# A four-layer graph stack on one core: TensorE's order written out for the third layer, with its side work cut into steps

## The chip, the cores and the metric

The kernel runs on one core of a Trainium2 chip. The metric is the device time of one execution in microseconds. Five engines work in parallel, each through its own queue in order: TensorE (PE in the profile, its weight loads PEld), VectorE (DVE), ScalarE (ACT), GpSimd (POOL) and SyncE (SP, which here only issues transfers). They wait for each other through semaphores.

## The reference

Four graph layers in a row over 4096 nodes with 256 features, all in float32. Each one adds an attention result to x and normalises every row (`x = layernorm(x + layer(x, adj))`). Which nodes see each other is given by a 4096 x 4096 integer matrix `adj`.

- Layer 0: additive attention with four heads, slope 0.2, then elu.
- Layer 1: dot-product attention with four heads of 64.
- Layer 2, the third layer: additive attention with one head:

```
h = x @ W;  e_src = h @ a[:D, 0];  e_dst = h @ a[D:, 0]
e = leaky(e_src[:, None] + e_dst[None, :], 0.01)
out = elu(softmax(where(adj > 0, e, -1e12), axis=1) @ h)
```

- Layer 3, the fourth layer: attention whose scores are cosines. `Qn` and `Kn` are the rows of `x @ Wq.T` and `x @ Wk.T` divided by their lengths, and the output is half the attended x plus half of x.

## The kernel before, in words

All of x stays in SBUF as `X`, 32 tiles of 128 nodes with 256 columns and one more for the sums. A row block is 512 nodes (`QW`), so there are `NB` = 8 row blocks b and `NT` = 32 column tiles j. The names below are those of the profile's lines.

**The third layer** (`additive_one`) goes through its units (b, j) with b outside and j inside. For a unit, `weights` loads the masks of two units with one transfer on SP's queue (L428), has ScalarE form `e` from the block's `row` (L430) and has VectorE multiply with the mask into `prob` (L432, three buffers). `sums` then does four matmuls, one for each 128 nodes of the block (L438), which add up in four PSUM banks over all j: for even b in banks of their own (`acc0` to `acc3`), for odd b in the rotating banks `g`. The loop emits `sums` of a unit one step after its `weights`.

Before it can use column tiles of a block, the block must be *prepared*: `turn` transposes its x tiles (L118) through two banks, VectorE and ScalarE copy one each into `xT` (L120), `additive_values` multiplies xT with the layer's weights in four banks (L177), and from each bank ScalarE takes three exponentials (L181 to L183) and VectorE the scaled values V (L184). Last, `row` of the block is filled: for blocks 0 and 1 by four transposes of `src` and a copy (L420, L421), for the later ones by two transfers on POOL's queue (L415, L416). Blocks 0 and 1 are prepared ahead of the loop and the others during row block 0, one every four units (at j = 2, 6, 10 and so on), each in one piece.

**The second layer's last outputs** (`tail` of `multi_head_attention`) are done inside the third layer, after `sums(0, 2)`: POOL adds the partial row sums (`join_sums`, L646), TensorE sums them over partitions (L658), ScalarE copies them (`kept`, L661), TensorE turns them (L666) and the outputs (L673), VectorE divides, adds to X and normalises. After it, `follow.start` opens the fourth layer's buffers and loads its weights.

**The fourth layer's preparations** (`Cosine.prepare`) for blocks 0 to 5 are done in the third layer's last row block (b = 7, at j = 2, 6 and so on) in the banks `acc` that are then free, and for blocks 6 and 7 in the fourth layer's first row block (at j = 1 and 12). Each turns x (L118), projects each of its four tiles (L795, two tiles share one bank), squares them with a running sum (`sq`, L799), copies a bank to `rows` (L801), works out the inverse root (L130 to L140), scales `rows` (L806), transposes them (L810) and copies the result to `T` (L811). Its main work is scores (L834), exponential (L837), mask (L838) and sums (L845).

**What sets the order.** In the first two layers TensorE's order is written out by hand (`tc.manual_schedule`). In the third and fourth a planner orders every engine's instructions by its own costs; the program's order is then a starting point. A tile that comes from a pool waits until the readers of the tile that had its buffer before are done.

## Time and profile before

| | us |
|---|---|
| median of three runs (2927.59 to 2929.03) | 2928.59 |
| the profiled execution's own time | 2932.88 |
| its span, first to last instruction | 2931.0 |
| third layer's front in it, 1724.5 to 1803.7 | 79.2 |
| its row blocks with no side work on TensorE, to 2154.9 | 351.2 |
| its last row block, to 2246.9 | 92.0 |
| fourth layer's front, to 2296.0 | 49.1 |

A line of the order in time has the start, the duration from the first start to the last end of a group of neighbours, engine, line, operation, output and inputs, the count, and in brackets the idle time before it with the engine and line that ended it. A float32 matmul leaves two records, a transpose one. Because matmuls are pipelined, a record's duration is longer than the distance to the next record's start. A line of the waits reads: who waited, for whom, microseconds in total, number of times, the longest.

### The profile page before, as it was taken

What the parts mean: (1) busy time and instruction counts of PE and PEld (TensorE: products, weight loads), DVE (VectorE), ACT (ScalarE), POOL (GpSimd) and SP (SyncE); (2) the same over time, 40 slices, a digit from 0 to 9 for tenths busy, and PEclk for the clock granted to TensorE, in tenths of its full rate; (3) what the DMA queues carried; (4) which work ended last, traced back from release to release, by engine and by line L of the source; (5) the groups of instructions that cost most, each with busy time, mean ns of one, the idle gap of its engine ahead of it and who ended that gap; (6) DMA issues with size and microseconds to landing.
All of it is one profiled execution on the core that took longest, in us unless ns stands there. A gap on an engine that the chain in (4) does not pass through costs nothing.

```text
span 2931.0 us, 50407 instructions
## 1 busy us (share of the span) xinstructions
PE 2909.7 (99%) x20269; PEld 1560.3 (53%) x20269; DVE 1958.3 (67%) x2545; ACT 1668.9 (57%) x2613; POOL 926.6 (32%) x647
## 2 busy tenths in 40 slices
PE   9999999999999999999999999999999999999998
PEld 4333333333643333333333358888887777777776
DVE  8899999997677777877877865555555333333333
ACT  7899999997356666666666654444444222222222
POOL 0010010100078888888889850000000000000000
PEclk9999999999999999999999999999999999999999
DMA  7566666664068888889889876444442333333331
GB/s 203 102 138 139 136 141 141 137 131 84 1 147 191 183 185 190 182 185 195 176 187 188 180 161 137 151 152 151 154 132 52 51 58 58 58 58 58 58 58 29
DMA packets 207148, 374.94 MB, mean 128 GB/s; under 512 B 15057, under 2 KB 90817, under 8 KB 206018
## 3 DMA queue, kind: packets, MB, share of 16 engines
q0 software_dynamic: 102304, 177.77, 38.3%
q1 hardware_dynamic: 104336, 193.69, 20.1%
q8 instruction: 159, 2.61, 0.4%
q14 instruction: 75, 0.61, 0.1%
q10 hardware_dynamic: 274, 0.26, 0.0%
HBM read 317.07 MB, written 21.04 MB: 115 GB/s over the span
## 4 chain that ended last, share of the span: by engine, by line
PE 96%; DVE 2%; ACT 0%; DMA 0%; SPq 0%; issue 0%; DVEq 0%; ACTq 0%
PE acc L274 23%; PE acc L845 15%; PE p L604 14%; PE acc L637 14%; PE g L438 8%; PE acc L438 8%; PE p L834 4%; PE g L834 3%; PE g L532 2%; PE g L177 1%; PE pv L546 1%; PE acc L795 1%; PE g L118 1%; DVE prob L616 1%; DVE s L139 1%; PE acc L177 1%
## 5 line engine op out<-in xcount | busy, mean ns | idle before, releaser
L616 DVE TENSOR_TENSOR prob<-p,mask 128x1024 f32<-128x1024 f32 x512 | 622.8, 1222 | 197.4 <-ACT p L606 193.6
L606 ACT ACTIVATE p<-p,shift 128x1024 f32<-128x1024 f32 x512 | 556.3, 1088 | 331.8 <-PE p L604 331.0
L274 PE MATMUL acc<-prob,V 128*32 128x512 f32 x6144 | 664.0, 592 | 1.1 <-DVE prob L264 1.1
L623 POOL TENSOR_TENSOR den<-den,prob 128x1024 f32<-128x1024 f32 x248 | 618.5, 2494 | 72.1 <-DVE prob L616 62.7
L261 ACT ACTIVATE prob<-row,dst 128x512 f32<-128x512 f32 x1020 | 633.1, 712 | 0.1
L264 DVE SCALAR_TENSOR_TENSOR prob<-prob,mask 128x2048 f32<-128x2048 f32 x256 | 582.4, 2286 | 24.2 <-ACT prob L261 20.6
L604 PE MATMUL p<-qT,kT 64*64 64x512 f32 x4096 | 532.7, 591 | 5.5 <-DVE prob L616 5.5
L637 PE MATMUL acc<-prob,V 64*64 64x512 f32 x4096 | 531.4, 589 | 0.0
L845 PE MATMUL acc<-X,prob 128*128 128x257 f32 x2048 | 486.0, 380 | 0.0
L845 PEld LDWEIGHTS acc<-X,prob 128*128 128x128 f32 x2048 | 388.4, 190 | 162.2 <-issue 113.5
L838 DVE TENSOR_TENSOR prob<-prob,mask 128x512 f32<-128x512 f32 x256 | 176.3, 691 | 419.5 <-ACT prob L837 418.4
L274 PEld LDWEIGHTS acc<-prob,V 128*32 128x32 f32 x6144 | 197.3, 110 | 453.0 <-issue 433.5
L91 POOL COPY tick<-prob 128x1 f32<-128x1 f32 x35 | 39.7, 1133 | 1019.9 <-DVE prob L264 646.0
L430 ACT ACTIVATE e<-row,dst 128x512 f32<-128x512 f32 x256 | 184.3, 721 | 241.2 <-DVE prob L432 208.4
L637 PEld LDWEIGHTS acc<-prob,V 64*64 64x64 f32 x4096 | 155.8, 133 | 285.4 <-issue 278.2
L604 PEld LDWEIGHTS p<-qT,kT 64*64 64x64 f32 x4096 | 153.6, 133 | 284.4 <-issue 255.8
L432 DVE SCALAR_TENSOR_TENSOR prob<-e,mask 128x512 f32<-128x512 f32 x256 | 178.3, 696 | 174.7 <-PE acc L438 92.9
L782 POOL DMA_DIRECT2D mask<-in_adjT x64 | 47.4, 741 | 639.5 <-DVE prob L838 509.7
L629 POOL DMA_DIRECT2D den<-prob x240 | 225.2, 938 | 28.5 <-DVE prob L616 21.9
L837 ACT ACTIVATE prob<-p 128x512 f32<-128x512 f32 x144 | 85.8, 596 | 256.7 <-PE p L834 242.7
L438 PE MATMUL g<-V,prob 128*128 128x257 f32 x1024 | 226.6, 380 | 0.0
L438 PE MATMUL acc<-V,prob 128*128 128x257 f32 x1024 | 225.3, 380 | 0.0
(154 smaller groups left out, 1973.7 us busy)
## 6 DMA issues: line engine op xcount, KB each, us to landing
mask<-in_adjT SPq DMA_DIRECT2D x256, 512.0 KB
den<-prob POOLq DMA_DIRECT2D x240, 512.0 KB, 5.3
mask<-edges SPq DMA_DIRECT2D x256, 128.0 KB
mask<-in_adjT POOLq DMA_DIRECT2D x64, 512.0 KB, 5.7
edges<-in_adj POOLq DMA_DIRECT2D x32, 512.0 KB, 9.9
den<-prob SPq DMA_DIRECT2D x16, 512.0 KB
row<-far SPq DMA_DIRECT2D x7, 1024.0 KB
X<-in_x SPq DMA_DIRECT2D x7, 512.0 KB
```

Of the source, the lines that this page charges most:

```text
L261: nc.scalar.activation(z[:, h, :], r, AF.Relu, bias=-1.0, scale=dst[:, j, h:h + 1])
L264: nc.vector.scalar_tensor_tensor(z, z, 1.0, mask[m][:, j % MJ, :].unsqueeze(1).to_broadcast([P, H, QW]), OP.add, OP.mult)
L274: nc.tensor.matmul(acc[b][h * G:(h + 1) * G, n, :], part, prob[b, j][:, h, :], start=(j == 0), stop=(j == NT - 1))
L438: nc.tensor.matmul(acc[b][k][:, :D + 1], prob[b, j][:, k * P:(k + 1) * P], V[:, j, :], start=(j == 0), stop=(j == NT - 1))
L604: nc.tensor.matmul(p[c * d:(c + 1) * d, r, :], kT[half, c, j * d:(j + 1) * d], qT[half, c, cols], start=True, stop=True)
L606: nc.scalar.activation(p, p, AF.Exp, bias=shift)
L616: nc.vector.tensor_tensor(z, p, mask[m][:, j % MJ, :].unsqueeze(1).to_broadcast([P, KC, QW]), OP.mult)
L623: nc.gpsimd.tensor_tensor(to, to, flat, OP.add)
L629: nc.gpsimd.dma_start(to, flat, accum_op=OP.add)
L637: nc.tensor.matmul(acc[b][c][r * d:(r + 1) * d, :], V[half, j, r * d:(r + 1) * d], prob[b, j][half, r, :], start=(j == 0), stop=(j == NH - 1))
L834: nc.tensor.matmul(p, T[:, 0, j * P:(j + 1) * P], T[:, 1, cols], start=True, stop=True)
L845: nc.tensor.matmul(acc[b][k], prob[b, j][:, k * P:(k + 1) * P], X[:, j, :], start=(j == 0), stop=(j == NT - 1))
```

## The change

TensorE's order in the third layer is now the program's own, through `tc.manual_schedule`; the other engines are still ordered by the planner. The program's order is changed with it:

- `prepare` of the third layer is split into `turn`, `project` and `fill_row`. A block's `turn` is emitted at j = 0, 4, 8 and so on, its `project` and `fill_row` two units later. In front of the loop, the projection of block 1 is split around the filling of row 0, and row 1 is filled after `sums(0, 1)`.
- `tail` of the second layer has three steps: POOL's additions after `sums(0, 0)`, the row sums after `sums(0, 3)`, the rest after `sums(0, 5)`, there with all transposes ahead of the reciprocals. `follow.start` comes after the last step. The tile for the row sums is taken where they are made.
- `Cosine.prepare` has three steps, at units 0, 2 and 5 of a period of four in the last row block and at (0, 1), (0, 3), (0, 6) and (0, 12), (0, 14), (0, 17) in the fourth layer: turn; projections, squares, root and scaling; transposes to T. In the middle step both tiles of a bank are projected before the first of them is squared.

```diff
+            with tc.manual_schedule(engines={mybir.EngineType.PE}):
+                xTs = {0: turn(0), 1: turn(1)}
+                project(0, xTs[0])
+                project(1, xTs[1], [0, 1])
+                fill_row(0)
+                project(1, xTs[1], [2, 3])
+                for i in range(len(units) + 1):
+                    if i < len(units):
+                        b, j = units[i]
+                        weights(b, j)
+                        if b == 0 and j // QB + 2 < NB:
+                            n = j // QB + 2
+                            if j % QB == 0:
+                                xTs[n] = turn(n)
+                            elif j % QB == 2:
+                                project(n, xTs[n])
+                                fill_row(n)
+                    if i:
+                        b, j = units[i - 1]
+                        sums(b, j)
+                        if (b, j) == (0, 1):
+                            fill_row(1)
+                        if b == 0 and j in (0, 3, 5):
+                            tail(bank, (0, 3, 5).index(j))
+                            if j == 5:
+                                follow.start()
...
+                            for step, first in enumerate((0, 2, 5)):
+                                if j >= first and (j - first) % 4 == 0 and (j - first) // 4 < NB - 2:
+                                    follow.prepare(even_bank, (j - first) // 4, step)
...
-        def tail(bank):
+        def tail(bank, step):
             b = NB - 1
-            join_sums(b, 1, nc.gpsimd)
-            join_sums(b, 2, nc.gpsimd)
-            row_sums(bank, b)
-            reciprocals(turned_row_sums(bank, b), b)
-            for k in (0, 2):
-                half(turned_half(bank, b, k), b, k)
...
+            if step == 0:
+                join_sums(b, 1, nc.gpsimd)
+                join_sums(b, 2, nc.gpsimd)
+            elif step == 1:
+                row_sums(bank, b)
+            else:
+                pd = turned_row_sums(bank, b)
+                pos = {k: turned_half(bank, b, k) for k in (0, 2)}
+                reciprocals(pd, b)
+                for k, po in pos.items():
+                    half(po, b, k)
...
+            if step == 0:
+                self.xT[b] = transposed_block(in_, bank, b)
+            elif step == 1:
...
+                for k in range(0, QB, 2):
                     pr = bank().rearrange("p (t n f) -> p t n f", t=2, f=P)
+                    for t in range(2):
+                        for c in range(KC):
+                            nc.tensor.matmul(pr[:, t, :, :], xT[:, c, (k + t) * P:(k + t + 1) * P], w_sb[:, c, :],
+                                             start=(c == 0), stop=(c == KC - 1))
+                    for t in range(2):
+                        for n in range(2):
+                            sq = in_.tile([P, P], FP, name="sq")
+                            nc.scalar.activation(sq, pr[:, t, n, :], AF.Square, accum_out=norm[:, k + t, n:n + 1])
+                    nc.vector.tensor_copy(rows[:, k:k + 2], pr)
...
+            steps = {(0, j + n): (NB - 2 + b, step) for b, j in enumerate((1, 12)) for step, n in enumerate((0, 2, 5))}
...
+                    if (b, j) in steps:
+                        co.prepare(bank, *steps[b, j])
```

## The prediction

> **What bounds the kernel now.** I read the page's busy times and its chain first: is one engine the limit, and where does it rest?

> ```profile
> PE 2909.7 (99%) x20269; PEld 1560.3 (53%) x20269; DVE 1958.3 (67%) x2545; ACT 1668.9 (57%) x2613; POOL 926.6 (32%) x647
> PE 96%; DVE 2%; ACT 0%; DMA 0%; SPq 0%; issue 0%; DVEq 0%; ACTq 0%
> ```

> TensorE is busy nearly all of the span and is 96% of the chain that ended last. So nothing is gained by making another engine faster; only TensorE's own standstills can be won. The matmul count is unchanged by the edit. Next, the windows table by stage (columns: PE, PEld, DVE, ACT, POOL busy with counts, granted clock, DMA share, GB/s), cut where the third layer's front (preparations in row block 0), its middle, its last row block and the fourth layer's front begin and end:

> ```profile
> 1724.50:1803.70 79.20, 77.08 (x405) 64.90 (x402) 42.67 (x87) 33.34 (x134) 11.55 (x12) 1.00 0.54 123
> 1803.70:2154.90 351.20, 351.20 (x1621) 307.37 (x1620) 196.20 (x430) 157.37 (x243) 1.83 (x3) 1.00 0.47 153
> 2154.90:2246.90 92.00, 91.67 (x450) 74.31 (x449) 51.86 (x123) 46.63 (x162) 3.54 (x7) 1.00 0.36 92
> 2246.90:2296.00 49.10, 48.68 (x204) 35.10 (x203) 26.32 (x66) 19.97 (x64) 2.22 (x3) 1.00 0.23 33
> ```

> The clock is 1.00 in all four, so it is no issue. Busy time misleads here: records of neighbouring matmuls overlap (each is 0.38 us long but the next starts 0.22 later), so a standstill under 0.2 us doesn't show as idle. I therefore count from start to start. TensorE's order in time gives the undisturbed pace:

> ```profile
> 1803.62 18.38 PE L438 MATMUL acc<-V,prob 128*128 128x257 f32 x84
> 1821.84 28.35 PE L438 MATMUL g<-V,prob 128*128 128x257 f32 x130
> ```

> 84 records in 18.22 us: 0.217 each (a float matmul leaves two records, a transpose one). In the same way L177 and L795 run at 0.217 and 0.216 where nothing holds them, and transposes at 0.109. Multiplying:
> - Front, from the first transpose (1724.51) to 1803.62: 172 records of L438 = 37.3, 128 of L177 = 27.9, 84 transposes (L118, L420, L666, L673) = 9.2, L658 = 0.6; sum 75.0. It took 79.1: **about 4.2 us stand still** (adding up single gaps gives 4.4).
> - Last row block, 2154.92 to 2246.89: 256 of L438 = 55.5, 96 of L795 = 20.7, 96 transposes = 10.5; sum 86.7. It took 92.0: **5.3** (gap by gap 5.6).
> - Fourth layer's front to 2296: gap by gap **1.7**.
> - The middle: 0.5 over 351 us, nothing to win.

> What ends these standstills is in the chain of waits, window 1690 to 2300, for TensorE and its weight loads:

> ```profile
> PE g L177 <- DVE xT L120: 1.9, 1, 1.9
> PE g L666 <- ACT kept L661: 0.2, 1, 0.2
> PEld acc L795 <- ACT sq L799: 3.9, 12, 0.4
> PEld acc L795 <- ACT xT L120: 1.7, 6, 0.4
> PEld g L795 <- ACT sq L799: 1.6, 4, 0.7
> ```

> A weight load that waits 0.2 to 0.4 is partly covered by the matmul still running; about 0.1 us shows on TensorE for each.

> **Part 1: block 2's turn two units ahead of its projection.** The one long wait, in order of time:

> ```profile
> 1736.46 2.34 POOL L646 TENSOR_TENSOR den<-den 128x1024 f32<-128x1024 f32 x1 [7.60 <-DMA den<-prob]
> 1736.55 2.81 DVE L432 SCALAR_TENSOR_TENSOR prob<-e,mask 128x512 f32<-128x512 f32 x1 [1.14 <-PE acc L438]
> 1739.28 0.68 DVE L120 COPY xT<-g 128x512 f32<-128x512 f32 x1
> 1740.11 3.91 PE L177 MATMUL g<-w_sb,xT 128*128 128x258 f32 x16 [1.85 <-DVE xT L120]
> ```

> VectorE's masking took 2.81 beside a usual 0.69 while POOL's addition ran; the copy of xT stood behind it, and TensorE behind the copy. In the changed order I place TensorE by its pace: turns of blocks 0 and 1 to 1726.25, project(0) to 1729.8, half of project(1) to 1731.5, row 0 to 1732.0, the other half to 1733.7, turn(2) to 1734.6, sums(0,0) to 1736.3, project(2) to 1739.8, sums(0,1) to 1741.5. VectorE in the built order: prob(0,0) ends 1734.3 (row copy 0.59 from 1732.3, e 0.72, prob 0.69), 0.3 before sums(0,0); xT(2) ends 1735.6, 0.7 before project(2); prob(0,1) then runs to 1736.3 and prob(0,2) meets POOL's addition.

> [...] By the rows, that prob ends 1739.4 at the latest, while project(2) needs none and keeps TensorE at work until 1739.8. I take 0 for it, 2.1 as the other end, and so **gain 2.0** (gap of 2.01).

> The same part also spaces the later turns (gaps of about 0.15 at each of blocks 4 to 7, 0.26 at block 2: 0.9 in all). **Gain 0.9.** Row fills inside the projections (four gaps, 0.44) go, since 4 x 0.217 x 2 of projection now lie between src and its transposes. **Gain 0.4.**

> **Part 2: the second layer's tail in three steps.** Row sums at (0,3), their transposes at (0,5): the wait for the two kept copies (0.36+0.11 start to start, and 0.1+0.1 around the sums) falls under two units of 1.73 us. **Gain 0.6.** Behind it VectorE gets reciprocals 0.3, two products 1.3, two additions 1.3, statistics of four rows 2.4, xT(4) 0.7, 6.0 in one burst before prob(0,9); from the last transposes TensorE has sums(0,6) to (0,8), turn(4) and project(4), 9.6 us, before it needs that prob: no wait. The two weight loads of SP's queue (0.37 and 0.46) wait for the row sums to free den, 1747 before and 1746.9 after by the pace; SP's list is the same, the mask behind them is for units 14 and 15, some 20 us later: 0. POOL's far and row transfers keep their order and feed row blocks from 2 on: 0.

> Front: 2.0+0.9+0.4+0.6 = **3.9** of 4.4.

> **Part 3: the fourth layer's preparations in steps, tiles of a bank ahead of squares.** One of six in the last row block:

> ```profile
> 2199.39 1.04 PE L118 MATMUL acc<-ident,X 128*128 128x128 f32 x8
> 2200.26 1.03 PE L438 MATMUL g<-V,prob 128*128 128x257 f32 x4
> 2201.13 3.07 PE L795 MATMUL acc<-w_sb,xT 128*128 128x256 f32 x12
> 2204.04 1.46 PE L438 MATMUL g<-V,prob 128*128 128x257 f32 x6
> 2205.49 1.13 PE L795 MATMUL acc<-w_sb,xT 128*128 128x256 f32 x4
> 2206.46 4.50 PE L438 MATMUL g<-V,prob 128*128 128x257 f32 x20
> 2211.01 1.06 PE L810 MATMUL acc<-ident,rows 128*128 128x128 f32 x8
> 2211.91 0.60 PE L438 MATMUL g<-V,prob 128*128 128x257 f32 x2
> 2212.34 1.04 PE L118 MATMUL acc<-ident,X 128*128 128x128 f32 x8
> ```

> From transposes to transposes 12.95 us. By the pace: 32 x 0.217 + 16 x 0.109 + 16 x 0.216 = 12.13. So 0.82 stands still: about 0.18 at xT's two halves, 0.36 at squares, 0.21 ahead of L810, the rest scattered. After: xT has two units (3.5 us) for two copies of 0.68 and 0.57: gone. A bank's eight records follow each other: gone.

> [...] The row: in the trace, the last projection's start to the end of the rows' scaling takes 4.6, with one prob in between; four squares in a row instead of two add 0.5: 5.1. The new order puts three units and a turn, 3 x 1.73 + 0.87 = 6.1, between. [...] Only the first preparation, where VectorE also does block 6's four outputs, comes out late. Its queue, from the block's start: first output and the taking of block 6 to 2.6, xT and probs 2 to 4 to 5.6, the other outputs (1.5 each, waiting for ScalarE's exponentials) around the copies of rows, which end at 12.6, prob(7,6) to 13.5, root to 14.5, scaling to 15.8; TensorE arrives at 15.6. With 0.2 to start, **0.4 is lost** (0 to 1.0). Gain in the last row block: 5.6 less 0.4 there, less 0.1 left of scattered gaps = **5.1**.

> In the fourth layer the planner still places TensorE. Steps at units 1, 3, 6 and 12, 14, 17 cover the same waits: of 1.7, I take **1.3** (0.5 to 1.7), as VectorE also finishes the third layer there.

> **Sum.** 3.9+5.1+1.3 = 10.3 of the profiled execution, whose time was 2932.88 (span 2931.0): 0.351%. The runs' median is 2928.59, 0.15% below it; the same share gives **2918.3 us**.

> **Rivals.**
> 1. [...] If prob(0,0) or xT(2) is still unserved at 1736.5 (0.9 of delay does it), project(2) or sums(0,1) waits as before: 2.1 back, and some 0.5 more where probs run late behind it: 2920.9. For it: the margins of 0.3 and 0.7 at sums(0,0) and project(2) are thin. Against: the addition's start is set by a transfer, not by VectorE.
> 2. *Short gaps are the price of a first weight load behind a wait, satisfied or not.* Then only the long ones go (2.0, 0.5, L810's 0.2 x 6, fourth layer 0.7): 4.4, so 2924.2. For it: gaps of 0.104 to 0.105 recur at every bank. Against: L438 waits for a prob in every unit of the middle and shows no gap.
> 3. *VectorE's chain to the rows becomes the bound: slower.* TensorE's order is now rigid; where before other matmuls were put in front of a late rows tile, it would stand. Each of eight preparations would pay what the chain exceeds 6.1 by; from 1.3 us of excess each, all 10.3 are gone, and at 2.2, a chain of 8.3, it is 2935.9. Against: VectorE has 6.9 us of work in 12.1 there (four probs 2.8, three copies 2.1, scaling 1.2, five small 0.8).
> 4. *The edit is void for other engines*, as it fixes TensorE alone. But the built order of VectorE and ScalarE does follow: xT's copy stands two or three probs ahead of its projection's values.

> **How the numbers follow.** The likeliest has 0.73, with its own range 2916.5 (all but 0.5 of 11.7 won, 11.2, and run noise of 0.7) to 2920.5 (first preparation 1.0, fourth layer 0.5, scattered). Rival 1 has 0.12, rival 2 0.10, rival 3 0.05. About 0.2% (5.9 us) is what a measurement of this kernel can tell from no change. The likeliest and rival 1 are faster by more, rival 2 is within it, rival 3 slower: 0.85, 0.10, 0.05. The range takes in rival 1: 2916.0 to 2922.5, leaving out rivals 2 and 3 and thin tails.

> **What would show it.** After: no wait of L177 for DVE's xT above 0.2; no weight load of a projection held by squares; transposes to transposes 12.1 to 12.2 for five of six preparations; one short wait at the first rows; the middle unchanged; the fourth layer beginning some 9 earlier. A prob of 2 to 3 us beside POOL's addition will still be there, with no TensorE wait after it. It would be wrong if gaps of 0.1 stay at satisfied waits, or if new waits for prob appear behind V's values or the tail's burst.

## The result, and the profile after

| | us, median | runs |
|---|---|---|
| before, beside the first runs of the changed kernel | 2928.45 (2927.59 to 2930.18) | 6 |
| changed | 2919.78 (2918.81 to 2921.05) | 6 |
| changed kernel's profiled execution (before: 2932.88) | 2920.01, span 2918.1 | 1 |

The ratio is 0.997, 95% interval 0.9957 to 0.9983: the change makes the kernel faster by 0.3%, 8.7 us. Measured a second time, with the kernel before beside it, it was 2920.49 against 2930.47, ratio 0.9965 (0.9953 to 0.9978), 10.0 us.

The page of the changed kernel, busy times and the chain that ended last:

```profile
PE 2901.0 (99%) x20269; PEld 1564.5 (54%) x20269; DVE 1959.0 (67%) x2545; ACT 1668.3 (57%) x2613; POOL 927.0 (32%) x647
PE 97%; DVE 2%; ACT 0%; issue 0%; DMA 0%; DVEq 0%; SPq 0%
```

The same number of matmuls, and the other engines are as busy as before. TensorE still sets the end; it only stands less. The windows table of the changed kernel, cut at the four stages (columns as before: length, then busy times with counts of PE, PEld, DVE, ACT, POOL, granted clock, DMA share, GB/s):

```profile
1722.75:1801.00 78.25, 78.25 (x418) 68.56 (x415) 43.59 (x90) 33.88 (x138) 12.97 (x14) 1.00 0.49 135
1801.00:2149.30 348.30, 348.30 (x1608) 304.80 (x1608) 195.04 (x427) 156.37 (x239) 0.54 (x1) 1.00 0.47 152
2149.30:2236.00 86.70, 86.70 (x450) 76.78 (x449) 52.41 (x123) 47.13 (x161) 3.62 (x7) 1.00 0.38 98
2236.00:2285.00 49.00, 49.00 (x206) 36.85 (x205) 26.87 (x67) 18.98 (x63) 2.37 (x4) 1.00 0.23 33
```

In each stage TensorE's busy time is now the whole length (before: 77.08 of 79.20 and 91.67 of 92.00). Busy time hides short standstills, so the count from start to start decides: 0.4 us stand still in the front and 0.15 in the last row block and the fourth layer's front together, where before it was 4.4 and 7.3. In the chain of waits from 1690 to 2320 there is no line left for TensorE, and of its weight loads none that waits for xT or sq.

The front in order of time, TensorE, VectorE and POOL, at the place of the former long wait:

```profile
1731.97 1.04 PE L118 MATMUL g<-ident,X 128*128 128x128 f32 x8
...
1733.11 0.68 DVE L120 COPY xT<-g 128x512 f32<-128x512 f32 x1
...
1734.58 3.66 PE L177 MATMUL g<-w_sb,xT 128*128 128x258 f32 x16
1735.17 2.35 POOL L664 TENSOR_TENSOR den<-den 128x1024 f32<-128x1024 f32 x1 [8.07 <-DMA den<-prob]
1735.24 2.83 DVE L434 SCALAR_TENSOR_TENSOR prob<-e,mask 128x512 f32<-128x512 f32 x1 [0.25 <-ACT e L432]
```

The prob beside POOL's addition still takes 2.83 us. But xT of block 2 was copied at 1733.11, before it, and TensorE is at work on the projection until 1738.08, about when VectorE is free again.

One preparation of the last row block, TensorE in order of time, from one turn to the next:

```profile
2174.42 1.04 PE L118 MATMUL acc<-ident,X 128*128 128x128 f32 x8
2175.30 1.90 PE L440 MATMUL g<-V,prob 128*128 128x257 f32 x8
2177.03 1.04 PE L840 MATMUL acc<-ident,rows 128*128 128x128 f32 x8
2177.91 1.90 PE L440 MATMUL g<-V,prob 128*128 128x257 f32 x8
2179.64 3.62 PE L823 MATMUL acc<-w_sb,xT 128*128 128x256 f32 x16
2183.09 3.63 PE L440 MATMUL g<-V,prob 128*128 128x257 f32 x16
2186.56 1.04 PE L118 MATMUL acc<-ident,X 128*128 128x128 f32 x8
```

12.14 us from turn to turn, where it was 12.95; the undisturbed pace gives 12.13. The sixteen projections now stand in one group.

### Where the time went

By TensorE's records I cut every trace at the same events: the start of the first transpose of the third layer, of the first sums of row block 1 (the front lies between), of the first sums of row block 7 and of the first record behind the last sums of that row block, and the end of TensorE's last record. In us:

| kernel | front | middle | last row block | rest (fourth layer) | sum |
|---|---|---|---|---|---|
| before | 97.32 | 333.08 | 91.98 | 676.06 | 1198.44 |
| before, second execution (first experiment) | 99.07 | 333.08 | 92.01 | 675.91 | 1200.07 |
| changed | 93.46 | 333.08 | 86.71 | 674.06 | 1187.31 |
| changed, second execution | 93.46 | 333.08 | 86.71 | 674.06 | 1187.31 |

The changed kernel gives the same numbers to a hundredth both times. The kernel before doesn't: its front differs by 1.75 us from one execution to another. The middle, which nothing touches, is equal in all. What the two profiled executions differ by beyond the 11.1 of this table (2932.88 - 2920.01 = 12.9) lies ahead of the third layer, in code that is the same; that start lay between 1721.6 and 1724.5 us over all traces of all kernels here, and the 1724.5 is the first trace of the kernel before.

### The profile page after: what moved, and what is told of

It reads as the page before. It is cut to its first block, busy times and chain, and to the rows that moved or that the text cites. A ratio compares the mean times of both kernels' runs of the same rounds, so it can differ in the third digit from the quotient of the medians.

```text
span 2918.1 us, 50377 instructions
## 1 busy us (share of the span) xinstructions
PE 2901.0 (99%) x20269; PEld 1564.5 (54%) x20269; DVE 1959.0 (67%) x2545; ACT 1668.3 (57%) x2613; POOL 927.0 (32%) x647
## 4 chain that ended last, share of the span: by engine, by line
PE 97%; DVE 2%; ACT 0%; issue 0%; DMA 0%; DVEq 0%; SPq 0%
PE acc L274 23%; PE acc L875 15%; PE p L622 15%; PE acc L655 14%; PE acc L440 8%; PE g L440 8%; PE p L864 4%; PE g L864 3%; PE g L550 2%; PE g L177 1%; PE pv L564 1%; PE g L118 1%; PE acc L823 1%; PE acc L177 1%; DVE prob L634 1%; DVE s L139 1%
## 5 line engine op out<-in xcount | busy, mean ns | idle before, releaser
L432 ACT ACTIVATE e<-row,dst 128x512 f32<-128x512 f32 x256 | 184.2, 722 | 235.1 <-DVE prob L434 209.0
```

## The experiments

My theory: TensorE's standstills come from dependences that are too close in its order; moving the dependent work some units away removes them, and the fixing of the order is only a means. Rivals: short gaps are the price of any wait, the gain is in one part alone, the fixed order itself is what helps.

### The kernel before, once more

The kernel before, unaltered.

> The kernel before, unchanged, profiled once more. The traces differ by 11.1 us from the third layer's first transpose to the end (1206.5 before, 1195.4 after), the runs' medians by 8.7. Theory A, the trace of before is typical: that stretch is 1206.5 again, with a wait of L177 for VectorE's xT of about 1.9 us. Theory B, the wait hangs on when the transfer ahead of POOL's addition lands, and differs between executions: the stretch comes out up to 2.5 us shorter, with a smaller wait or none.

Measured 2930.82 us, ratio to the other runs of before 0.9999 (0.9991 to 1.0007). Its trace in order of time, POOL, VectorE and TensorE at the long wait:

```profile
1733.98 2.35 POOL L646 TENSOR_TENSOR den<-den 128x1024 f32<-128x1024 f32 x1 [7.65 <-DMA den<-prob]
1734.01 2.86 DVE L432 SCALAR_TENSOR_TENSOR prob<-e,mask 128x512 f32<-128x512 f32 x1 [1.14 <-PE acc L438]
...
1737.62 5.59 PE L177 MATMUL g<-w_sb,xT 128*128 128x258 f32 x16 [1.90 <-DVE xT L120]
```

and the windows of this trace over that projection (the granted clock is the third value from the end):

```profile
1737.60:1738.70 1.10, 1.08 (x3) 0.78 (x4) 0.00 (x0) 0.56 (x2) 0.00 (x0) 0.79 0.76 149
1738.70:1741.80 3.10, 3.10 (x9) 2.42 (x9) 0.69 (x2) 0.59 (x6) 0.00 (x0) 0.52 0.32 116
1741.80:1745.00 3.20, 3.20 (x16) 2.79 (x15) 1.70 (x4) 0.69 (x7) 0.62 (x1) 1.00 0.02 5
```

The same wait of 1.9 us again (idle 1.90 here, 1.85 in the first trace). The addition came 12.0 us after the layer's first transpose, as in the first trace. Yet the front was 1.75 longer, and the windows say why: behind the wait the granted clock was 0.52 for three microseconds. The projection came at half the pace, 0.43 from record to record instead of 0.217, and its sixteen records took 5.59 in place of 3.91. In the first trace of the same program the clock stayed at 1.00 there (1740.1 to 1744.3). So this one collision has no fixed price: 2.0 in one execution, 3.8 in another. Neither theory had this; the last section works out from the traces how the two executions differ.

### The front alone

The changed kernel's front (turns early, tail in steps, order fixed), with the old preparations of the fourth layer, whose row block is again ordered by the planner:

```
-                            for step, first in enumerate((0, 2, 5)):
-                                if j >= first and (j - first) % 4 == 0 and (j - first) // 4 < NB - 2:
-                                    follow.prepare(even_bank, (j - first) // 4, step)
+                            if j % 4 == 2 and j // 4 < NB - 2:
+                                follow.prepare(even_bank, j // 4)
...
+                for i in range((NB - 1) * NT):
+                    unit(i)
+            for i in range((NB - 1) * NT, len(units) + 1):
+                unit(i)
```

> The change in row blocks 0 to 6 alone (turn, project, fill_row apart, the second layer's tail in steps, TensorE's order fixed there); the fourth layer's preparations in one piece as before, ordered by the planner. Theory: the front's standstills go (4.4 to 0.4 by the trace after), so 4.0 us faster than before if the wait for xT is in every execution, 2.0 if it is not; the last row block keeps its 5.3. Rival, that VectorE's and ScalarE's planned order in the last block follows the front: it changes there too.

Measured 2927.45 us, ratio 0.9989 (0.9983 to 0.9996) to before at 2930.8: 3.35 less. Front 93.46, last row block 92.01. The whole front is won, not only its long wait, and nothing leaks into the last row block.

### The fourth layer's preparations alone

The kernel before with only the preparations in three steps and both tiles of a bank ahead of the squares; the planner orders TensorE:

```
-                    if b == NB - 1 and j % 4 == 2 and j // 4 < NB - 2:
-                        follow.prepare(even_bank, j // 4)
+                    if b == NB - 1:
+                        for step, first in enumerate((0, 2, 5)):
+                            if j >= first and (j - first) % 4 == 0 and (j - first) // 4 < NB - 2:
+                                follow.prepare(even_bank, (j - first) // 4, step)
```

> The other part alone: the fourth layer's preparations in three steps with both tiles of a bank ahead of squares, no order fixed, the front as before. Theory: 7.2 us faster than before, since the gaps of the last row block and of the fourth layer's front (7.3) go to 0.15, and the planner keeps the steps' order; the front keeps 4.4. Rival, that the fixed order is what wins there: the planner moves the projections back among the sums, and at most half of it, 3 us, is won.

Measured 2923.64 us, ratio 0.9975 (0.9965 to 0.9985): 7.16 less. Last row block 86.71, the same as in the changed kernel, with no order fixed; front 96.61, the old one. So the steps do it. The two parts add up in the traces: the front of the run above is that of the changed kernel, and so is the last row block of this one. The medians' 3.35 + 7.16 = 10.5 stands beside 8.7 and 10.0 for the whole change. Built without the fixed order, the whole changed program also comes out with the same list of instructions on all five engines: once the program's order is spaced, the planner keeps it, in the front too.

### Squares between the tiles of a bank

The changed kernel with one line left out, so that the first tile of a bank is squared before the second is projected:

```
                             for c in range(KC):
                                 nc.tensor.matmul(pr[:, t, :, :], xT[:, c, (k + t) * P:(k + t + 1) * P], w_sb[:, c, :],
                                                  start=(c == 0), stop=(c == KC - 1))
-                    for t in range(2):
                         for n in range(2):
```

> The changed kernel with each tile's squares ahead of the next tile of its bank again. In the third layer TensorE's order doesn't change, so the second tile of a bank waits for two squares of the first. Theory, by the trace of before (squares start 0.41 after the last record of a tile starts, take 0.26 + 0.36 with the read of the sum, then a weight load): 0.9 to 1.0 of standstill twice per preparation, 11 us over six, which takes back the whole change: 2930 to 2932. Rival, that a wait for squares costs only the 0.10 seen before: 2921.

Measured 2935.63 us, ratio to before 1.0017 (1.0011 to 1.0024): slower than before. In its chain of waits, and on TensorE in order of time within one preparation:

```profile
PE acc L823 <- ACT sq L827: 11.8, 12, 1.3
```

```profile
2183.16 1.03 PE L823 MATMUL acc<-w_sb,xT 128*128 128x256 f32 x4
2185.47 1.99 PE L823 MATMUL acc<-w_sb,xT 128*128 128x256 f32 x8 [1.28 <-ACT sq L827]
2188.24 1.13 PE L823 MATMUL acc<-w_sb,xT 128*128 128x256 f32 x4 [0.78 <-ACT sq L827]
```

The last row block grew by 15.0, 1.25 for each of twelve waits, not the 0.95 that I expected. The second wait of a pair is that size (start to start 0.94 over the pace), the first is 1.45, because the forming of `e` for a unit of the main work (0.72) stood ahead of the squares on ScalarE. In the kernel before the same dependence cost 0.36 for each preparation, because the planner had put sums between the tiles. A fixed order needs this edit: without it the last row block loses 15.0, more than the whole change wins.

### Rows one unit, and two units, after the projections

In the changed kernel three units lie between the projections and the transposes of the scaled rows. Two kernels with one number different:

```
-                            for step, first in enumerate((0, 2, 5)):
+                            for step, first in enumerate((0, 2, 3)):
```

> The changed kernel with one number different: in the third layer's last row block the third step (rows transposed to T) comes one unit after the projections, not three. Theory A (the distance of the steps is what hides VectorE's and ScalarE's chain): in the changed kernel this chain takes 4.97 us from the start of the last projection to the end of the scaling (5.3 in the first preparation), and about 0.15 more to TensorE's start. With one unit between them (1.75 of projection and unit, 0.2 of the last projection itself) TensorE arrives after 1.95 and stands 3.2, six times: 19 us more than the changed kernel in the last row block (86.7 becomes 105.8), some 2939 in all, slower than before by about 0.3%. Theory B (rival 3 of the prediction the other way round: the chain is short when nothing else is in VectorE's queue, so the distance does not matter): last row block 87 to 90, total within 3 us of the changed kernel, about 2920 to 2923.

Measured 2950.09 us, ratio to before 1.0063 (1.0049 to 1.0078). Its chain of waits, and its windows around one wait:

```profile
PE acc L840 <- DVE rows L834: 15.0, 5, 3.0
PE acc L840 <- DVE s L137: 3.3, 1, 3.3
```

```profile
2176.00:2182.00 6.00, 3.35 (x16) 2.61 (x14) 3.66 (x9) 3.36 (x19) 0.96 (x2) 1.00 0.32 87
2182.00:2187.00 5.00, 4.64 (x19) 4.02 (x20) 0.33 (x2) 1.17 (x2) 0.00 (x0) 0.66 0.77 108
2187.00:2194.00 7.00, 7.00 (x37) 6.23 (x36) 2.56 (x4) 3.69 (x12) 0.00 (x0) 1.00 0.37 99
```

The waits are as predicted by theory A: 3.17 from start to start, five times, and 3.47 the first time, 19.3 in all. The last row block grew by 29.6 to 116.30, though. The rest, 10.3 or 1.7 for each wait, is in the second window: the granted clock is 0.66 there and back at 1.00 in the third. After every one of the six waits nine or ten records took double their usual distance (sums 0.43 instead of 0.217).

The same number again, two units instead of three, `(0, 2, 4)`:

> The changed kernel with the third step of the preparations in the last row block two units after the projections, not three (one unit gave 116.3 us for the last row block instead of 86.7: 3.17 us of waiting each time, and behind each wait about 1.5 us more because TensorE's next records came at half the pace, the granted clock being 0.58 to 0.69 there). Between the projections and the rows lie two units and the next turn, 0.2 + 3.46 + 0.87 = 4.5 us (3.7 for the last preparation, which has no turn behind it), against a chain of 4.97 (5.28 in the first) and 0.15. Theory A (a wait costs its own length, and below about 1.3 us the clock stays up, as it did with waits of 1.25): waits of 0.9, four of 0.6 and one of 1.4, 4.7 us in all, last row block 91.4, granted clock 1.00 throughout, time about 2925. Theory B (every standstill is followed by matmuls at half the pace): 1.5 more for each wait, last row block about 100, granted clock under 0.97 there, time about 2934.

Measured 2924.93 us, ratio to before 0.9981 (0.9973 to 0.9988), last row block 91.41, and the clock 1.00. Its chain of waits:

```profile
PE acc L840 <- DVE rows L834: 2.9, 5, 1.3
PE acc L840 <- ACT xT L120: 0.7, 1, 0.7
```

Theory A holds to 0.01 us: 4.70 more than the changed kernel. Each wait is what the chain (4.97, and 0.15 to TensorE's start) exceeds the work in between by, and with these standstills, of up to 1.43, the granted clock was 1.00 over the block.

### POOL's second addition left out

The kernel before without this instruction, which leaves one part of the row sums of the second layer's last block out:

```
             join_sums(b, 1, nc.gpsimd)
-            join_sums(b, 2, nc.gpsimd)
```

> The kernel before, with one instruction left out: POOL's second addition in the second layer's last outputs (the one of 2.34 us beside which VectorE's prob took 2.81). One part of the row sums of that layer's last block is thereby missing. Everything else, TensorE's order too, is as before. Theory A (the wait of 1.9 for xT is made by that addition, through VectorE): no prob longer than 0.8 us and no wait of L177 for xT at this place; the front takes 96 to 97 us where the two looks at the kernel before took 97.3 and 99.1; time 1.5 to 2.5 us under the kernel before. Theory B (the wait is that of the turn itself: TensorE arrives too early for the copies whether or not POOL works): a wait of L177 for xT of 1 to 2 us stays, and the time is within 0.7 us of the kernel before.

Measured 2929.55 us against 2931.33, ratio 0.9995 (0.9986 to 1.0003). Its trace at the place:

```profile
1736.30 0.69 DVE L432 SCALAR_TENSOR_TENSOR prob<-e,mask 128x512 f32<-128x512 f32 x1 [1.14 <-PE acc L438]
1736.91 0.68 DVE L120 COPY xT<-g 128x512 f32<-128x512 f32 x1
1737.84 3.81 PE L177 MATMUL g<-w_sb,xT 128*128 128x258 f32 x16
```

The prob takes 0.69 and the wait for xT is gone, in TensorE's old order: the addition made the wait, through VectorE. The front is 95.21, where I expected 96 to 97. That is below the three old fronts with the addition (96.61, where the held prob took 2.09 and TensorE was idle for 1.13; 97.32; 99.07) and still 1.75 over the new one: the short gaps at the turns (0.15 each), at row fills (0.24) and at the kept copies (0.37) are there as before. By the time alone this run can't be told from no change; the trace tells it.

### The tail in one piece

The changed kernel with the second layer's last outputs in one piece again:

```
-                        if b == 0 and j in (0, 3, 5):
-                            tail(bank, (0, 3, 5).index(j))
-                            if j == 5:
-                                follow.start()
+                        if (b, j) == (0, 2):
+                            for step in range(3):
+                                tail(bank, step)
+                            follow.start()
```

> The changed kernel with the second layer's last outputs in one piece again, all three steps one behind the other after sums(0, 2), TensorE's order fixed as in the changed kernel. Theory A (part 2 of the prediction: the steps hide the kept copies): a wait of TensorE for kept comes back, 0.36 and 0.11 and two of 0.1, so the front takes 94.0 to 94.4 instead of 93.46 and the time is 0.6 to 0.9 us over the changed kernel, about 8 under the kernel before. Theory B (the tail's early position also lets VectorE's burst and POOL's addition fall on other probs, and TensorE pays for that): the front grows by 2 us or more, and new waits for prob or for POOL's den stand in it.

Measured 2921.28 us, ratio to before 0.9966 (0.9954 to 0.9979), front 94.81. The one line of its chain of waits:

```profile
PE g L685 <- ACT kept L680: 1.3, 1, 1.3
```

The mechanism is theory A's, and nothing of theory B shows; the size is 1.35 by the front instead of 0.5 to 0.9. I had taken the wait of the kernel before, where the planner had put sums of a unit between the row sums and their transposes; in a fixed order nothing stands there. The medians (0.8 over the changed kernel's second median, 1.5 over its first) are too close to tell more.

### The order fixed, nothing else

The kernel before with only its TensorE order in the third layer fixed, as the program has it:

```
+            with tc.manual_schedule(engines={mybir.EngineType.PE}):
                 for b, xT in enumerate([turn(0), turn(1)]):
                     prepare(b, xT)
```

> The kernel before with TensorE's order in the third layer fixed to its own program order, and nothing cut into steps: the first line of the change alone. Theory A (the gain is in the distance of the steps; fixing alone takes away what the planner put in between): in each of six preparations of the last row block TensorE waits for xT (about 0.9), twice for squares between the tiles of a bank (1.2 each) and for the whole chain to the scaled rows (4.6, of which 0.2 lies under the last projection), 7.7 in all, where 0.9 stood before: 6 x 6.8 = 41 us more in the last row block (92 becomes 133); in the front each of eight turns is followed by its projection at once, 0.9 each, so 3 to 7 more; in all about +46, 2976, between 2960 and 2990. Theory B (the written order was the main part of the change, because the planner's own order was worse than the program's): faster than before, 2920 to 2927.

Measured 2991.18 us, ratio 1.0204 (1.019 to 1.0219). Lines of its chain of waits:

```profile
PE acc L811 <- DVE rows L807: 25.5, 6, 4.4
PE acc L796 <- ACT sq L800: 9.0, 12, 0.8
PE acc L796 <- ACT e L430: 3.5, 5, 0.7
...
PE g L667 <- ACT kept L662: 1.3, 1, 1.3
```

Theory B falls by a wide margin, and theory A was too low: the last row block took 146.06, 54 more than before, where I expected 41, and the front 5.3 more, as expected. The waits are as listed (4.4 for rows, 0.9 twice for squares, 0.9 ahead of the first projection), and from start to start the block's standstills grew by 40.7. Missing in my sum was the clock again: the other 13.4 us are 48 transposes that came at 0.21 instead of 0.109, and 34 sums and six projections at 0.43. Over the whole block the granted clock was 0.87. The six projections stand ahead of the first wait of 4.4: there the clock had fallen behind waits of 0.9 and 0.7 alone.

### The changed kernel, once more

> The changed kernel once more, unaltered, on one chip with the run below and with the kernel before. Theory A (the gain is the sum of the parts, 3.35 measured for the front and 7.16 for the fourth layer's preparations alone): 10.5 us under the kernel before in this job. Theory B (the parts overlap, and the two medians of the first result are right): 8.7 under it. In the trace no wait of TensorE in the third layer and a front of 93.46, as the first time.

Measured 2920.49 us, 10.0 under the kernel before beside it: nearer to the sum of the parts, 10.5, though the interval (6.4 to 13.8) holds 8.7 too. Front, middle and last row block were as in the first trace.

No kernel of these is faster than the changed one. There's also little left for one to win here: 0.6 us of standstill from the first turn to the fourth layer's front.

## Why the prediction was right, point by point

2918.3 was predicted, and the medians are 2919.78 and 2920.49, in the likeliest case's own range.

**The sum, against the profiled execution.** Front 3.9 predicted, 97.32 - 93.46 = 3.86 measured. Last row block 5.1 predicted, 5.27 measured. Fourth layer 1.3 predicted, 2.0 measured (the steps there hid all of the standstill, and I had kept 0.4 back for VectorE's work at the end of the third layer). Together 10.3 and 11.1.

**Carrying it over to the medians** leaves the largest difference: they are 1.5 and 2.2 above the prediction. It isn't clear of noise, since a gain of 10.3 lies in both intervals (5.0 to 12.6 and 6.4 to 13.8 us). I took the share 0.351% of one execution of 2932.88, 4.3 above its kernel's median, to hold for the median. But the old front isn't the same in each execution: 96.6, 97.3 and 99.1 in three traces, by the length of the held prob (2.09, 2.81, 2.86) and by whether the clock falls behind the wait (0.52 in the last); the new front is 93.46 each time. So the price of the long wait that I read, 2.0, was that of one execution, and that it was neither the lowest nor the highest of the three was luck. The gain was 8.7 and 10.0 by the medians, 11.1 by the two traces. The 4.3 itself is not the front's: the second execution had the longer front and was faster, 2931.97, because it reached the third layer 2.5 us earlier. The second time the kernel before itself had a median of 2930.47, 1.9 above the 2928.59 that the prediction started from. How often an execution meets which front no run shows, since of each kernel's executions side by side only one leaves a trace.

**Part 1, the prob beside the addition.** The addition still met a prob: 2.83 beside 2.35 in the changed kernel, where it had been 2.81 beside 2.34 before. The 2.1 that I put at the other end is what this prob took over its usual 0.69. No run shows that this length has to come back at another prob; in the changed kernel it did, at one. What I took, 0 instead of 2.1, was right, and with more room than I gave it. I had prob(0,2) meet the addition; VectorE was one ahead, so it was the fourth prob of the row block, (0,3), which ended at 1738.07 and was needed by the sums at 1742.86. TensorE arrived where I placed it: 7.0 us after the first turn at row 0 by the estimate and in the trace, 15.3 at the end of project(2) in both. Leaving the addition out confirmed the cause, 0.69 instead of 2.8, and in the second execution of the kernel before the wait of 1.90 cost 3.8, with the granted clock at 0.52 behind it.

**Part 2.** With the order fixed, the steps are worth 1.35, twice the 0.6 that I read from the planner's order. The two are not the same comparison: 0.6 is what I read in the old order, 1.35 what the new one would pay without the steps. Of the 0.6, about 0.5 was won, at the kept copies (0.36 and 0.11). The two gaps of 0.1 before and behind the row sums stand in the changed kernel too (0.09 and 0.10), so they were no wait for the copies.

**Part 3, squares and the chain.** The preparation period is 12.14 as predicted (12.1 to 12.2). The squares came later, as the new order has them: the first of a bank started 1.93 after its projections (2167.50 to 2169.43) where before it was 1.26 (2201.13 to 2202.39), and the chain from the last projection to scaled rows went from 4.62 to 4.97; I had 5.1. TensorE came to the rows 1.32 after the scaling was done, where my 6.1 less 5.1 left 1.0: I had also left out the last projection itself, 0.2. That holds for four of the six preparations. The first had 1.0, and the last 0.45, since no turn stands behind it. The steps with one unit and with two units show that this distance is real: there the chain comes out on TensorE, to 0.01 us.

**The step that failed** is the loss of 0.4 at the first preparation. I had the scaling end 15.8 after the block's start and TensorE arrive at 15.6; it arrived at 15.6, but the scaling had ended at 14.6. I had added up VectorE's durations. Neighbouring records of VectorE overlap in the changed kernel's trace, as TensorE's do; at the end of this chain,

```profile
2161.17 0.16 DVE L831 TENSOR_SCALAR v<-norm 128x8 f32<-128x8 f32 x1
2161.24 0.69 DVE L434 SCALAR_TENSOR_TENSOR prob<-e,mask 128x512 f32<-128x512 f32 x1
```

where the second starts 0.07 after the first, whose record is 0.16 long. From the block's start to the end of the scaling VectorE's 44 records add up to 17.9 us; they overlap by 4.7 and leave 1.3 idle. Half of my 1.2 arose before the copies of rows ended (12.0, where I had 12.6), half behind them. How much of it is overlap and how much the place I gave to single instructions, no run parts.

**The rivals.** That project(2) or sums(0,1) waits as before (2920.9) has a time as near to the first median as the likeliest case, so the time can't tell them apart. The trace does: no TensorE wait follows the held prob. That short gaps are the price of a satisfied wait is refuted: the front alone won 3.35 and the steps alone 7.16, and of the gaps of 0.1 only the two at the row sums are left, which end no wait of TensorE in the list. VectorE's chain as the bound didn't come, with 0.45 to 1.3 us to spare in the last row block, but one unit less between projections and rows costs 4.7 us, and two less 29.6. The void edit is refuted by the front alone and by the preparations alone.

## What to carry to other kernels

Where one engine is the bound at 99%, count its standstills from start to start against its own undisturbed pace, and put the next dependent step further away than the chain behind it is long; the distances can be read from the trace to a tenth of a microsecond. Fixing an order by hand brings nothing in itself: here the planner writes the same list once the steps are there, and without them the fixed order costs 60 us. Behind a standstill of 1.90 us in one execution, and behind two of 0.90 and 0.72 close together, the granted clock was 0.50 here, so standstills can be worth more than their length, and their price in one profiled execution is no measure of the median.

## What the runs showed of the hardware that was not expected

The granted clock of the traces goes with this. It is recorded as 1.00 or 0.50 (a mean such as 0.66 is a stretch that holds both). In the second execution of the kernel before it was 0.50 for 3.41 us behind the wait. In the first traces of the kernel before and of the changed kernel it was 1.00 for 2914.982 and 2904.742 us on end, until 3.6 and 3.3 us ahead of the last instruction's end; that is 854 and 851 times 3.4133. I therefore cut the traces into stretches of 3.41 us, laid so that the recorded changes of the clock fall on their borders, and counted TensorE's work in each, every record with its undisturbed pace, twice that at half clock. That such stretches mean anything where the clock doesn't change is my estimate from these lengths. From the third layer on the clock went from 1.00 to 0.50 once in the second execution of the kernel before, six times with the rows one unit away, seven times with the fixed order alone and once at each kernel's end, and by this count the stretch ahead held 1.18 us of work or less each time. Three examples, as windows of the profile (PE busy first, the granted clock third from the end): the kernel before in its first execution, in its second with the stretch behind, and the fixed order alone with the stretch behind:

```profile
1736.16:1739.58 3.42, 2.10 (x14) 1.56 (x12) 3.03 (x2) 0.15 (x2) 2.34 (x1) 1.00 0.23 83
...
1734.83:1738.24 3.41, 1.51 (x8) 0.75 (x6) 2.65 (x2) 1.19 (x2) 1.49 (x1) 1.00 0.11 23
1738.24:1741.65 3.41, 3.41 (x9) 2.76 (x9) 0.55 (x2) 0.59 (x6) 0.00 (x0) 0.50 0.45 137
...
2166.02:2169.43 3.41, 1.79 (x7) 0.90 (x7) 2.65 (x9) 2.24 (x7) 0.00 (x0) 1.00 0.73 224
2169.43:2172.84 3.41, 3.16 (x8) 1.99 (x6) 2.68 (x8) 1.20 (x6) 0.00 (x0) 0.50 0.02 7
```

In the first execution the wait of 1.85 lies across the border of two stretches, 1.3 us in this one; 1.93 us of work are left, and the clock behind it is 1.00. In the second the wait of 1.90 falls into one stretch whole, 1.18 are left, and the clock behind it is 0.50, then 1.00 again from 1741.80 on. In the third the two short waits leave 1.09, and the clock behind them is 0.50. (Busy time is higher than these counts, since a record is longer than its pace.) That an execution meets the first or the second case by where its stretches happen to lie is my estimate from these two traces; no run sets it. 3.41 us at half the pace, with TensorE at work all through, cost 1.7: this agrees with the 1.75 of the second execution and the 1.7 behind each wait with the rows one unit away.
